# Summing pairs of state products with an accumulating transfer before TensorE adds them, in the selective-scan stage of a four-layer network

## The chip, the cores and the metric

The kernel runs on one core of one Trainium2 chip. The metric is the device time of one execution in microseconds, median over several runs. Everything is computed in float32.

## The reference, cut to what matters

The network has four layers, each an attention-like part and a feed-forward part with a residual and a layer norm. The change lies in the last layer's first part, a selective state-space recurrence. With 4 batches of 1024 tokens, 256 channels `e` and 16 states `n` it computes

```python
def step(h, inp):
    d_l, b_l, c_l, x_l = inp
    h = jnp.exp(d_l[:, :, None] * A) * h + (d_l * x_l)[:, :, None] * b_l[:, None, :]
    y_l = jnp.einsum('ben,bn->be', h, c_l)
    return (h, y_l)
_, ys = lax.scan(step, h0, (delta, Bm, Cm, xs))
y = ys.transpose(1, 0, 2) + xs * W_D
```

So for each state `n` there is a linear recurrence over the tokens for every channel. Its result is multiplied by `C[n]`, and the 16 products are summed. After that come a gate, a projection, a layer norm, and the last feed-forward part, a mixture of eight experts of width 512 that are all computed and weighted by a gate.

## The kernel before, in words

The program is written with pools of named tiles. Each pool has a number of buffers per name. A scheduler that estimates times fixes the order of the instructions on each engine when the program is built; on the chip each engine then works through its own queue in that order, and semaphores hold an instruction until its inputs are there and its output buffer is free.

The last layer is worked off in eight halves: four batches, two halves of 512 tokens each. Three pieces of code make up a half:

- `l3_prepare` (L1613) norms the input, projects it (`pxe`), applies the convolution, projects to delta, B and C (`pdb`, then `pd`), and leaves `dl` (delta, 128 channels x 2 x 512), `ud` (delta times x, the same shape) and, in DRAM, `rows`: 16 rows of B and 16 of C. The last matmuls of it on TensorE (PE) are `pd` at L1694; VectorE (DVE) writes `ud` at L1709.
- `l3_scan` (L1713) loops over the 16 states. For each it loads a row of B and a row of C, broadcast to 128 partitions, on SyncE's queue (`bn` and `cn`, L1734, 256 KB each, four buffers). GpSimd (POOL) multiplies `ud` with `bn` into `db` (L1739, four buffers). ScalarE (ACT) makes the decay `da` with an exponential (L1743). DVE runs the recurrence along the tokens in place in `db` (L1744). POOL multiplies `db` with `cn` into `hc` (L1755, 128 x 1024, 512 KB, four buffers). PE sums: with an identity as the fixed matrix, two matmuls per state, one per 128 channels, add `hc` into two PSUM banks `pys` that stay open over the 16 states (`add`, L1724, recorded at L122, the line of the helper `mm`). The add of state `n - 1` is issued after the product of state `n`.
- `l3_finish` (L1766) gates and projects the result, norms it, and puts the half on a list for the last feed-forward part.

`l3` (L1514) weaves them: while the scan of a half is written down state by state, each step also takes one piece of the preparation of the next half, one piece of the finish of the half before and some pieces of side work. The side work (`l3_side`, L1565) is first the rest of the mixture of experts of the layer before (with its gathers by POOL, `yg`, L1468), then `l3_ffn` (L1835), the last feed-forward part of halves that are finished: matmuls `ph`, Relu on ACT (`hh`, L1848), matmuls `py`, and a weighted sum on DVE (`h_acc`, L1864). What is left of it after the last scan ends the program.

Of the kernel before, what the change touches and what calls it, by code (L numbers as in the profile page):

```python
# [14 lines left out]
ALU = mybir.AluOpType  # L15
# [25 lines left out]
E3, NST, DDELTA, KCONV = 256, 16, 64, 4  # L41
# [17 lines left out]
class Net:  # L59
# [1653 lines left out]
    def l3_scan(self, u):  # L1713


        nc, c3, b, h = self.nc, self.c3, u["b"], u["h"]
        sp, wp, aneg = c3["sp"], c3["wp"], c3["aneg"]
        wout = c3["we"][:, :, ND:]
        xnT, xs, dl, ud, rows = (u[k] for k in ("xnT", "xs", "dl", "ud", "rows"))
        carry = wp.tile([P, 2, NST], F32, name="carry") if h == 0 else u["prev"]["carry"]  # L1720
        u["carry"] = carry
        py = [self.psb(f"y{ec}", [P, 512], f"pys{ec}") for ec in range(2)]

        def add(n, hc):  # L1724
            for ec in range(2):
                self.mm(py[ec], self.ident, hc[:, ec, :], n == 0, n == NST - 1)

        last = None
        for n in range(NST):
            bc = []  # L1730
            for i, nm in enumerate(("bn", "cn")):
                t = wp.tile([P, 1, 512], F32, name=nm, bufs=4)
                r = i * NST + n
                nc.sync.dma_start(  # L1734
                    out=t[:, 0, :], in_=rows[r : r + 1, :].to_broadcast([P, 512])
                )
                bc.append(t.to_broadcast([P, 2, 512]))
            db = wp.tile([P, 2, 512], F32, name="db", bufs=4)
            nc.gpsimd.tensor_mul(db, ud, bc[0])  # L1739
            for ec in range(2):  # L1740
                j = ec * NST + n
                da = self.psb("da", [P, 512], "da")
                nc.scalar.activation(da, dl[:, ec, :], AF.Exp, scale=aneg[:, j : j + 1])  # L1743
                nc.vector.tensor_tensor_scan(  # L1744
                    db[:, ec, :],
                    da,
                    db[:, ec, :],
                    carry[:, ec, n : n + 1] if h else 0.0,
                    ALU.mult,
                    ALU.add,  # L1750
                )
            if h == 0:
                nc.scalar.copy(carry[:, :, n : n + 1], db[:, :, 511:512])
            hc = wp.tile([P, 2, 512], F32, name="hc", bufs=4)
            nc.gpsimd.tensor_mul(hc, db, bc[1])  # L1755
            if last is not None:
                add(n - 1, last)
            last = hc
            yield
        add(NST - 1, last)  # L1760
        for ec in range(2):
            nc.vector.scalar_tensor_tensor(
                xs[:, ec, :], xs[:, ec, :], self.col("W_D", i=ec), py[ec], ALU.mult, ALU.add
            )
# [317 lines left out]
```

## Time and profile before

| | us |
|---|---|
| median of 3 runs | 2528.93 |
| lowest, highest | 2528.28, 2533.65 |
| own time of the profiled execution | 2467.89 |
| its span, first to last instruction | 2466.1 |
| PE busy | 2154.3 (87%) |
| DVE busy, ACT busy | 1447.0 (59%), 1355.3 (55%) |
| POOL busy | 817.9 (33%) |
| `db` products on POOL, 128 of 2.37 us | 299.6 |
| `hc` products on POOL, 128 of 2.37 us | 299.8 |
| `pys` matmuls on PE, 512 records of 0.62 us | 247.1 |

A 512-wide float32 matmul leaves two records, so the 256 adds show as 512. Records of one engine overlap a little; back to back, one record follows another of this shape after 0.43 us. The profile is of one execution, on the core's own clock; PE's granted clock was 0.921 of full speed over the span. The scans begin at 1442.6 us, and the last `pys` add is at 2315.8 us.

### The profile page before, as it was taken

To read this page: it belongs to the slowest core of one execution; us is meant where nothing else is said; L and a number is where in the kernel's file an instruction comes from. 1 tells how busy PE (TensorE), PEld (TensorE's weight loads), DVE (VectorE), ACT (ScalarE), POOL (GpSimd) and SP (SyncE) were. 2 spreads that over 40 slices of the span, in tenths; PEclk is the share of its full clock that TensorE was granted. 3 is DMA by queue.
4 is the path that set the end of the run, shared out by engine and by line. 5 is a ranking of instruction groups with operands and counts; after the bars stand their busy time and mean duration, and the time that the engine had idled before them with its cause. 6 is when DMAs were issued, how large, how long until landed. Compare 5 with 4: busy or idle time off the path is not lost.

```text
span 2466.1 us, 34752 instructions
## 1 busy us (share of the span) xinstructions
PE 2154.3 (87%) x12026; PEld 1447.0 (59%) x12026; DVE 1447.0 (59%) x4119; ACT 1355.3 (55%) x2917; POOL 817.9 (33%) x509
## 2 busy tenths in 40 slices
PE   6677888888999999999999768866999999999988
PEld 2455654534677777777776434433566555555656
DVE  7448744323566756756665467767775657666431
ACT  6642433422666656565654676666756565656443
POOL 5002310000000020020012287778792938568300
PEclk9667989989999999999999978886999999899989
DMA  3001100001400000000002243343332222313000
GB/s 99 0 18 26 30 26 9 9 9 46 150 1 1 1 14 6 5 13 4 7 13 83 65 135 103 106 148 102 83 83 61 82 70 73 94 54 120 22 5 5
DMA packets 110431, 122.27 MB, mean 50 GB/s; under 512 B 15477, under 2 KB 72816, under 8 KB 109872
## 3 DMA queue, kind: packets, MB, share of 16 engines
q1 hardware_dynamic: 103728, 106.23, 14.9%
q0 software_dynamic: 5376, 9.62, 1.4%
q10 hardware_dynamic: 1152, 4.19, 0.5%
q8 instruction: 97, 1.59, 0.3%
q14 instruction: 78, 0.64, 0.1%
HBM read 96.85 MB, written 23.16 MB: 49 GB/s over the span
## 4 chain that ended last, share of the span: by engine, by line
PE 62%; DVE 18%; ACT 11%; issue 5%; DMA 3%; POOL 1%; SPq 0%; DVEq 0%; ACTq 0%; POOLq 0%
PE ph L122 13%; PE py L122 9%; PE pys L122 6%; PE po L1086 4%; PE po L122 4%; PE pt L126 3%; DVE db L1744 3%; PE pqk L122 3%; PE po L1102 3%; PE pr L122 2%; PE pv L122 2%; PE pst L122 2%; DVE num L1122 2%; DVE a L1075 1%; PE pa L122 1%
## 5 line engine op out<-in xcount | busy, mean ns | idle before, releaser
L1739 POOL TENSOR_TENSOR db<-ud,bn 128x1024 f32<-128x1024 f32 x128 | 299.6, 2373 | 187.4 <-DVE ud L1709 105.2
L1755 POOL TENSOR_TENSOR hc<-db,cn 128x1024 f32<-128x1024 f32 x128 | 299.8, 2371 | 41.7 <-DVE db L1744 26.6
L122 PEld LDWEIGHTS py<-wH,hh 128*128 128x128 f32 x2048 | 251.1, 193 | 77.3 <-issue 46.1
L122 PE MATMUL py<-wH,hh 128*128 128x128 f32 x2048 | 257.3, 278 | 11.5 <-ACT hh L1848 10.8
L122 PE MATMUL ph<-xT,wH 128*128 128x512 f32 x512 | 258.8, 623 | 7.0 <-DVE ln_nm L161 3.6
L122 PE MATMUL pys<-hc,sb_c_ident 128*128 128x512 f32 x512 | 247.1, 616 | 17.6 <-POOL hc L1755 17.6
L1122 DVE SCALAR_TENSOR_TENSOR num<-po,sb_c_trig,nsin 128x65 f32<-128x65 f32 x512 | 132.4, 278 | 210.9 <-ACT nsin L1119 210.5
L1119 ACT ACTIVATE nsin<-po,sb_c_trig 128x65 f32<-128x65 f32 x512 | 148.3, 316 | 188.9 <-DVE num L1122 113.3
L1848 ACT ACTIVATE hh<-ph,sb_cols 128x512 f32<-128x512 f32 x256 | 171.0, 681 | 136.3 <-PE ph L122 110.2
L1743 ACT ACTIVATE da<-dl,aneg 128x512 f32<-128x512 f32 x256 | 175.8, 690 | 84.4 <-DVE db L1744 83.5
L122 PEld LDWEIGHTS pys<-hc,sb_c_ident 128*128 128x128 f32 x512 | 97.6, 198 | 125.0 <-issue 104.1
L996 POOL MEMSET cv<- 128x16 f32 x32 | 4.0, 127 | 501.4 <-ACT cv L1013 310.6
L1744 DVE TENSOR_TENSOR_SCAN db<-da,db 128x512 f32<-128x512 f32 x128 | 149.3, 1206 | 31.0 <-POOL db L1739 16.6
L1744 DVE TENSOR_TENSOR_SCAN db<-da,carry,db 128x512 f32<-128x512 f32 x128 | 155.7, 1265 | 16.9 <-POOL db L1739 12.1
L1864 DVE SCALAR_TENSOR_TENSOR h_acc<-py,gt,h_acc 128x128 f32<-128x128 f32 x256 | 71.8, 342 | 136.6 <-PE py L122 136.4
L122 PEld LDWEIGHTS ph<-xT,wH 128*128 128x128 f32 x512 | 93.4, 200 | 93.5 <-issue 67.3
L122 PE MATMUL pqk<-xT,wE 128*128 128x256 f32 x512 | 137.4, 391 | 9.4 <-DVE cv L1006 6.1
L1338 POOL DMA_INDIRECT xrows<-xN,di x64 | 61.7, 964 | 235.8 <-ACT kN L1040 162.7
L1086 PE MATMUL po<-cv,a 128*128 128x130 f32 x1024 | 136.2, 275 | 1.9 <-DVE num L1122 1.9
L1086 PEld LDWEIGHTS po<-cv,a 128*128 128x128 f32 x1024 | 125.2, 191 | 3.9 <-PE pst L122 1.1
L126 PE MATMUL pt<-sb_c_ident,xN 128*128 128x128 f32 x256 | 64.4, 353 | 71.1 <-ACT xN L165 50.1
L122 PE MATMUL ph<-wF,xgT 128*128 x184 | 107.6, 671 | 13.5 <-ACT mhT L1435 7.8
(425 smaller groups left out, 4372.8 us busy)
## 6 DMA issues: line engine op xcount, KB each, us to landing
bn<-rows SPq DMA_DIRECT2D x128, 256.0 KB, 3.4
cn<-rows SPq DMA_DIRECT2D x128, 256.0 KB, 3.3
xrows<-zero SPq DMA_DIRECT2D x4, 1472.0 KB, 11.9
xg<-xrows SPq DMA_DIRECT2D x20, 256.0 KB, 2.9
yrows<-ys SPq DMA_DIRECT2D x20, 256.0 KB, 2.4
wH<-in_wH ACTq DMA_DIRECT2D x8, 512.0 KB, 6.4
wF<-in_wF SPq DMA_DIRECT2D x1, 3072.0 KB, 16.4
xN<-in_x SPq DMA_DIRECT2D x8, 256.0 KB, 4.7
```

The source lines that it names most:

```text
L122: return self.nc.tensor.matmul(out=out, lhsT=lhsT, rhs=rhs, start=start, stop=stop)
L126: self.nc.tensor.transpose(out, in_, self.ident[0:n, 0:n])
L1086: self.nc.tensor.matmul(out=u["po"][i][:, c, :], lhsT=u["a"][:, i, c, :], rhs=Q["v"][c][:, 2 * hp + i, :, :].rearrange("p a d -> p (a d)") ...
L1102: self.nc.tensor.matmul(out=u["po"][i][:, c, :], lhsT=u["q"][h, s], rhs=Q["st"][h, hp, c, :], start=False, stop=True, skip_group_check=True,)
L1119: nc.scalar.activation(t, po[i][:, c, VW : 2 * VW], AF.Copy, scale=trig[:, k, 1:2])
L1122: nc.vector.scalar_tensor_tensor(num[:, c, i, :], po[i][:, c, 0:VW], trig[:, k, 0:1], t, ALU.mult, ALU.add)
L1739: nc.gpsimd.tensor_mul(db, ud, bc[0])
L1743: nc.scalar.activation(da, dl[:, ec, :], AF.Exp, scale=aneg[:, j : j + 1])
L1744: nc.vector.tensor_tensor_scan(db[:, ec, :], da, db[:, ec, :], carry[:, ec, n : n + 1] if h else 0.0, ALU.mult, ALU.add,)
L1755: nc.gpsimd.tensor_mul(hc, db, bc[1])
L1848: nc.scalar.activation(ht, ph, AF.Relu, bias=self.col("h_b1", i=e * NK + k))
L1864: nc.vector.scalar_tensor_tensor(acc[:, c, :], py[:, c, :], gt[:, c, e : e + 1], acc[:, c, :], ALU.mult, ALU.add,)
```

## The change

The products of two states that follow each other are now added first. After the second of the two products, POOL issues a transfer from the second `hc` tile onto the first one (`prev`), which adds in place of overwriting (`accum_op=ALU.add`). PE then adds the first tile, which holds the sum, into `pys`. There are eight such adds per half in place of sixteen. The add of a pair is issued two states later than the pair's transfer, and those that are left are issued after the loop.

```diff
         def add(n, hc):
             for ec in range(2):
-                self.mm(py[ec], self.ident, hc[:, ec, :], n == 0, n == NST - 1)
-
-        last = None
+                self.mm(py[ec], self.ident, hc[:, ec, :], n == 1, n == NST - 1)
+
+        sums = []
+        prev = None
         for n in range(NST):
...
             hc = wp.tile([P, 2, 512], F32, name="hc", bufs=4)
             nc.gpsimd.tensor_mul(hc, db, bc[1])
-            if last is not None:
-                add(n - 1, last)
-            last = hc
-            yield
-        add(NST - 1, last)
+            if n % 2:
+
+                nc.gpsimd.dma_start(out=prev, in_=hc, accum_op=ALU.add)
+                sums.append((n, prev))
+            prev = hc
+            if sums and sums[0][0] <= n - 2:
+                add(*sums.pop(0))
+            yield
+        for p in sums:
+            add(*p)
```

Nothing else differs in the source. The scheduler sees other instructions, so the built order of the last stage differs on every engine.

## The prediction

> **What bounds the kernel now.** I read the engine totals first, then the last stage cut at the starts of its eight scans (one per half of a batch), then the chain, then the rows of what the change touches.
>
> ```profile
> PE 2154.3 (87%) x12026; PEld 1447.0 (59%) x12026; DVE 1447.0 (59%) x4119; ACT 1355.3 (55%) x2917; POOL 817.9 (33%) x509
> ```
> TensorE is the busiest engine overall. Now the stage: time, then PE, PEld, DVE, ACT and POOL busy, PE clock, DMA share, GB/s.
>
> ```profile
> core 0: us, PE busy (x) PEld busy (x) DVE busy (x) ACT busy (x) POOL busy (x), PEclk, DMA share, GB/s
> 1442.60:1536.70 94.10, 77.40 (x244) 40.20 (x245) 69.96 (x108) 62.20 (x137) 75.24 (x33) 0.85 0.41 115
> 1536.70:1673.70 137.00, 95.97 (x347) 53.68 (x348) 94.72 (x174) 86.73 (x185) 104.74 (x65) 0.83 0.40 125
> 1673.70:1771.50 97.80, 82.49 (x311) 45.90 (x310) 72.15 (x125) 69.51 (x128) 74.90 (x32) 0.85 0.32 89
> 1771.50:1895.00 123.50, 118.64 (x557) 76.24 (x555) 77.80 (x148) 76.21 (x124) 74.08 (x33) 0.99 0.26 71
> 1895.00:2014.70 119.70, 111.40 (x520) 69.97 (x520) 75.98 (x147) 77.11 (x143) 74.05 (x33) 0.99 0.28 76
> 2014.70:2125.50 110.80, 103.73 (x441) 62.53 (x440) 73.64 (x136) 66.98 (x112) 73.98 (x33) 0.92 0.29 80
> 2125.50:2231.40 105.90, 100.07 (x446) 61.66 (x445) 71.42 (x131) 65.65 (x115) 74.05 (x32) 0.97 0.28 83
> 2231.40:2316.00 84.60, 83.37 (x393) 53.04 (x391) 56.88 (x99) 48.37 (x74) 74.02 (x32) 1.00 0.25 75
> 2316.00:2466.00 150.00, 130.05 (x697) 91.87 (x696) 34.99 (x128) 58.88 (x94) 0.00 (x0) 0.92 0.02 6
> ```
> Two regimes. In halves 0 to 2 (beside the experts) PE is 70 to 84% busy and POOL 77 to 80%. From half 3 on PE is at 93 to 99%, while POOL needs a constant 74 us per half and then waits:
>
> ```profile
> 1836.25 9.31 POOL L1755 TENSOR_TENSOR hc<-db,cn 128x1024 f32<-128x1024 f32 x4
> 1894.96 9.30 POOL L1739 TENSOR_TENSOR db<-ud,bn 128x1024 f32<-128x1024 f32 x4 [49.40 <-DVE ud L1709]
> ```
> It idles 49 us because ud of the next half is late, and ud is late because its matmuls stand in PE's queue behind FFN work. So PE sets the late halves. One early wait goes the other way: PE stands for hc around the start of the third scan (waits from 1630 to 1700 us).
>
> ```profile
> PEld pys L122 <- POOL hc L1755: 19.0, 3, 14.7
> ```
>
> **What the Trainium skill says.** "DMA: Bandwidth & Descriptors", section "SWDGE vs HWDGE vs iDMA": a transfer that accumulates can be issued from GpSimd only, in software. No run here has one; the indirect gathers (L1468) are the nearest. "Collectives: The Full Stack", "The bandwidth ceiling: the fold count and why AG ≠ RS ≠ AR": an add in the DMA engine costs no cycles of its own, but needs two reads per write, so it runs at half the rate of a copy. No trace here shows it. The DMA page, "Anatomy of one DMA — SWDGE (gpsimd) path", prices such a transfer at 2.0 us plus bytes/436e3. The gather of 64 KB comes to 2.15 by this; the trace has 2.6, which I use.
>
> **The change part by part.** (1) Adds on PE. A state's add is four records of 0.43 us:
>
> ```profile
> 1846.88 1.72 PE pys L122 x4
> ```
> 128 states become 64 pairs: 64 x 1.72 = 110 us of PE work gone, 41 in halves 0 to 2 and 69 in halves 3 to 7.
>
> (2) The new transfer. Each of 64 reads 512 KB of hc and 512 KB of prev, and writes 512 KB. Its nearest rows:
>
> ```profile
> L1468 POOL DMA_INDIRECT yg<-yrows,di x64: 940/945/988, 1359.4 to 1668.8; - x64
> ...
> DMA to landing us min/median/max: 2.4/2.6/6.7
> ...
> orows<-vmr SPq DMA_DIRECT2D x4, 512.0 KB, 3.2
> ...
> rows<-db SPq DMA_DIRECT2D x8, 64.0 KB, 1.7
> ```
> Issue: 0.94 us plus the 0.30 between two, 1.25 us of POOL, 10 us per half. Upper bound 3 us (more descriptors per row, since two tensors are read); below 0.9 nothing here goes. Landing L, from issue: rows and orows give 1.5 us for 448 KB, 3.3 us per MB. From the 2.6 of a 64 KB gather, 960 KB more to read is 3.2: L = 5.8 alone. While a scan runs the loads of bn and cn hold about 0.44 of the DMA engines, so the same 3.2 becomes 5.7, L = 8.3. I take 7 and keep 5 to 12: an adder slower than a copy would be above 8.3.
>
> (3) What waits for it. POOL's built order in a late half is: transfer k, db, odd hc, db, even hc, transfer k+1. That even hc takes the buffer that transfer k reads (hc has four), so it waits for L. A pair takes 4 x 2.31 (9.3/4) + 1.25 = 10.5 us as long as L is below 1.25 + 3 x 2.31 = 8.2; above, L + 2.3. **This is the hinge.** Queued behind that even hc are the next transfer and all later db, then DVE's scans. PE's add waits for the landing, with FFN matmuls and the next half's pdb and pd behind it. ACT's order holds the exponentials of five states past a pair before the first Relu that depends on matmuls behind the pair's add, so a PE wait doesn't stop POOL.
>
> (4) Moves. The scheduler rewrites the order. Summing PE's rows with their durations (0.86 us per 512-wide matmul, 0.22 per 128-wide one), PE work from one half's pd to the next is, halves 3 to 4, 4 to 5, 5 to 6, 6 to 7: 119, 106, 94, 94 before; 104, 96, 76, 80 after. The next half's pd now stands after the sixth pair of eight (halves 3, 5, 6) or the eighth (4), where it stood after all sixteen states: next half's preparation starts earlier. In half 1, 14 gathers (14 x 1.25 = 17.5 us) stand ahead of one pair's transfer; the same gathers lay inside this scan before. ACT and DVE have the same work in another order; SP issues the same 256 loads, later where POOL is later, four buffers deep: no cost while POOL takes 10.5 us for the two states of a pair.
>
> **The sum**, L = 7, from pd to scan start 16 us (measured 14.4, 14.6, 17.7).
> - Starts of half 0 to half 3, 328.9 us: up to where PE waits for POOL, two halves of issues, 20, and one landing, 7: +27. From there to half 3's pd PE has 37 us of work in place of 57, times 1.15 (the late intervals run 4 to 18% over PE's work): -23. Net +4.
> - 3 to 4: 123.5 before. PE alone: 104 x 1.04 = 108. The loop by POOL: 16 + 78 (ten products and two issues to the first transfer, five pairs) + 7 + 10 of FFN ahead of pd = 111. Take 112.
> - 4 to 5: 119.7 before; loop 16 + 83 + 7 + 4 = 110.
> - 5 to 6 and 6 to 7: 110.8 and 105.9 before; PE 76 x 1.18 and 80 x 1.13, both 90; loop 16 + 71 + 7 + 3 = 97 each.
> - 7 to the end: 234.6 before; POOL 83 + 7 + 2, then the last FFN, 150 x 114/119 (PE work after the last add) = 144: 236.
>
> Late sum 652 against 694.5: -42. PE and POOL are now within 7 us of each other in every interval, so a delay of either shows; I add 4 us per half, 20. Total 4 - 42 + 20 = **-18 us**. Own time of the profiled execution 2467.9 (1.8 around the span of 2466.1): 2450. The median of the runs is 61 us above that; the same -18 gives **2511**.
>
> **Rivals.** (B) Transfer becomes the bound, slower. It decides at L = 8.4. Each us above 8.2 lengthens 29 late pair steps, 16 early ones and six landings, 51 us in all; from 7 to 8.2 only the landings grow (+7, to -11). L = 9.3 gives -11 + 56 = +45, 2574; L = 10 gives 2610. For: DMA share is already 0.40 in halves 0 and 1, and no row shows an adding transfer. Against: 5.8 alone, and bn and cn come in bursts.
> (C) Issue is dear: 3 us, so 1.75 x 45 steps = +79 on top, 2590. For: POOL would go from 74 to 98 us per half. Against: gathers of 128 rows take 0.94.
> (D) Freed PE time turns fully into waits for pairs: 2529. For: POOL's 84 us exceeds PE's 76 and 80 in the last halves. Against: the 30 to 49 us that POOL idles between scans now.
> (E) L = 5 and PE sets everything: late intervals 108, 108, 93, 93, 232 with no extra, -60, early +2, less some: 2475. That it doesn't do what it says is out: the built program has 128 matmuls of pys, not 256.
>
> **How the numbers follow.** A with E 0.48, of which 0.46 lie below -0.2%; D 0.10, 0.01 of it faster, 0.08 same; B 0.31; C 0.11, where 0.02 of these are same. Faster 0.47, same 0.10, slower 0.43; 0.2%, 5 us, is what this measurement can tell from no change (its runs span 5.4). Both signs hold much of the chance: A alone is 2478 to 2524. The range for all, 2480 to 2622, leaves out L above 10.2 and the lowest of E.
>
> **What would show it.** Right: pys at 256 records and about 110 us; transfers landing in 6 to 8 us, 1.25 us apart from POOL's work; POOL's idle before ud below 25 us per half; scan starts about 97 to 112 us apart. Wrong: even hc waiting for the transfer (a landing above 8.4), PE idle before pys by more than 5 us per pair, or scan starts over 115 us apart.

## The result, and the profile after

The changed kernel takes 2500.98 us (median of 4 runs, 2495.84 to 2507.25), the kernel before 2528.61 on the same chip: a ratio of 0.9888, with an interval of 0.986 to 0.9916, or 28 us less. The forecast was 18 us less.

The kernel before took about 2528 us in the first two series of runs and about 2468 us in the two later ones, as in its own profiled execution; some 50 us of that lie ahead of the first scan (1491.0 against 1442.6 us), so kernels are compared at the same level only (lower: 2468, upper: 2528), and why there are two levels is not known.

The engine totals and the DMA queue from the page of the changed kernel, in microseconds and share of the span:

```profile
PE 2087.7 (83%) x11770; PEld 1425.0 (57%) x11770; DVE 1460.1 (58%) x4119; ACT 1353.9 (54%) x2918; POOL 874.1 (35%) x573
...
q0 software_dynamic: 14592, 43.18, 8.3%
...
L122 PE MATMUL pys<-hc,sb_c_ident 128*128 128x512 f32 x256 | 135.4, 655 | 25.1 <-DMA hc<-hc 25.1
```
`pys` has half its records and 135.4 us in place of 247.1: 112 us of PE work are gone. PE's total fell by less, 91 us at the same level (2178.4 in a second profile of before), so the other matmuls took longer; the granted clock of the span was 0.893 in place of 0.910. The queue that only carried gathers (5376 packets, 1.4%) now has 14592 packets and 8.3%. The last number is new: PE stood 25 us for landings of the transfer (its weight loads, PEld, stood over much the same stretches).

The last stage of the changed kernel, cut at its scan starts; the columns are time, busy time of PE, PEld, DVE, ACT and POOL, PE clock, DMA share and GB/s:

```profile
1494.10:1584.20 90.10, 63.37 (x215) 34.45 (x216) 69.29 (x111) 69.11 (x147) 76.74 (x37) 0.80 0.54 144
1584.20:1742.70 158.50, 86.29 (x319) 49.41 (x317) 100.90 (x185) 92.21 (x193) 110.40 (x73) 0.74 0.49 134
1742.70:1839.00 96.30, 69.95 (x258) 39.69 (x258) 71.74 (x108) 57.19 (x107) 81.47 (x41) 0.81 0.57 139
1839.00:1958.20 119.20, 111.26 (x538) 72.89 (x539) 82.44 (x152) 76.18 (x127) 87.59 (x45) 0.99 0.50 123
1958.20:2075.80 117.60, 102.83 (x490) 67.24 (x489) 74.97 (x147) 77.10 (x142) 81.29 (x40) 0.93 0.45 113
2075.80:2174.40 98.60, 87.17 (x399) 55.25 (x398) 72.28 (x135) 66.28 (x112) 81.10 (x41) 0.93 0.53 132
2174.40:2268.90 94.50, 81.41 (x395) 52.62 (x394) 72.74 (x131) 63.80 (x112) 81.04 (x41) 0.92 0.54 137
2268.90:2364.80 95.90, 86.00 (x411) 56.09 (x410) 62.47 (x111) 54.34 (x87) 80.98 (x40) 0.94 0.46 113
2364.80:2505.00 140.20, 122.57 (x676) 88.14 (x674) 32.86 (x118) 53.72 (x84) 0.00 (x0) 0.93 0.02 4
```
In the late halves PE has fallen from 93 to 99% of the interval to 86 to 93%, and POOL has gone from 74 to 81 to 88 us per half. In the last three halves both now stand at about 81 to 87 us of 95 to 99. The share of the DMA engines went from 0.28 to about 0.5.

The intervals against the forecast. The lower level pairs the profile of before (span 2466.1) with a second profile of the changed kernel (span 2443.3); the upper level pairs a second profile of before (span 2529.3) with that of the changed kernel (2505.3).

| us | forecast | before, after (lower level) | change | before, after (upper level) | change |
|---|---|---|---|---|---|
| half 0 to 3 | +4 | 328.9, 335.9 | +7.0 | 339.8, 345.0 | +5.2 |
| 3 to 4 | -11.5 | 123.5, 119.2 | -4.3 | 122.1, 119.2 | -2.9 |
| 4 to 5 | -9.7 | 119.7, 115.6 | -4.1 | 122.4, 117.6 | -4.8 |
| 5 to 6 | -13.8 | 110.8, 99.7 | -11.1 | 111.1, 98.6 | -12.5 |
| 6 to 7 | -8.9 | 105.9, 94.6 | -11.3 | 106.2, 94.5 | -11.7 |
| 7 to the end | +1.4 | 234.6, 235.9 | +1.3 | 236.7, 236.4 | -0.3 |
| allowance | +20 | | | | |
| sum | -18.5 | | -22.5 | | -27.0 |

POOL in a late half of the changed kernel (start and duration in us):

```profile
1906.26 2.36 POOL L1756 TENSOR_TENSOR hc<-db,cn 128x1024 f32<-128x1024 f32 x1
1908.57 0.83 POOL L1759 DMA_DIRECT2D hc<-hc  x1
1909.15 2.65 POOL L1740 TENSOR_TENSOR db<-ud,bn 128x1024 f32<-128x1024 f32 x1
1911.47 2.62 POOL L1756 TENSOR_TENSOR hc<-db,cn 128x1024 f32<-128x1024 f32 x1
1913.79 2.62 POOL L1740 TENSOR_TENSOR db<-ud,bn 128x1024 f32<-128x1024 f32 x1
1916.11 2.61 POOL L1756 TENSOR_TENSOR hc<-db,cn 128x1024 f32<-128x1024 f32 x1
1918.40 1.16 POOL L1759 DMA_DIRECT2D hc<-hc  x1
1918.97 2.96 POOL L1740 TENSOR_TENSOR db<-ud,bn 128x1024 f32<-128x1024 f32 x1
```
The record of the issue lasts 0.8 to 1.2 us, and the next product starts 0.58 us after it (1908.57 to 1909.15), so the records overlap. But that is not all that the issue costs. The products behind it last longer, 2.65 us in place of 2.36, and 2.96 behind the next transfer. These later ends are real, for what depends on a product starts with them: here a scan on DVE starts 0.03 us after a product that lasted 3.05 us (the bracket is the idle time before, with what ended it).

```profile
1754.78 3.05 POOL L1740 TENSOR_TENSOR db<-ud,bn 128x1024 f32<-128x1024 f32 x1
1757.86 2.34 DVE L1745 TENSOR_TENSOR_SCAN db<-da,db 128x512 f32<-128x512 f32 x2 [5.30 <-POOL db L1740]
```
From the product behind one transfer to that behind the next are 9.82 us by their starts and 10.13 by their ends (1911.80 to 1921.93), and four products without a transfer take 9.25. So an adding transfer costs POOL about 0.9 us, 0.58 of which show in the starts. The busy time agrees: 81.1 us per half in place of 74.0 is 7.1 for eight transfers.

Waits of the changed kernel, first PE up to 1842 us (halves 0 to 2), then POOL from there to the last scan's end (who waited for whom: us in all, times, longest):

```profile
PE pys L122 <- DMA hc<-hc: 22.9, 4, 10.9
```
```profile
POOL db L1740 <- ACT dl L1710: 36.3, 2, 26.1
POOL db L1740 <- DVE ud L1709: 29.9, 2, 19.9
POOL hc L1756 <- PE pys L122: 19.5, 7, 5.1
```
Of PE's 25 us, 23 lie before half 3; in the late halves it hardly stands for a landing. POOL's idle time for the next half's `dl` and `ud` is 66 us over four halves there, where before it was 163. The third line is new there: the product that takes over the tile with a pair's sum waits until PE has read it.

### The profile page after: what moved, and what is told of

Its sections match the earlier page's. It is cut to its first block, busy times and chain, and to the rows that moved or that the text cites. A ratio compares the mean times of both kernels' runs of the same rounds, so it can differ in the third digit from the quotient of the medians.

```text
span 2505.3 us, 34222 instructions
## 1 busy us (share of the span) xinstructions
PE 2087.7 (83%) x11770; PEld 1425.0 (57%) x11770; DVE 1460.1 (58%) x4119; ACT 1353.9 (54%) x2918; POOL 874.1 (35%) x573
## 3 DMA queue, kind: packets, MB, share of 16 engines
q0 software_dynamic: 14592, 43.18, 8.3%
## 4 chain that ended last, share of the span: by engine, by line
PE 59%; DVE 18%; ACT 11%; issue 6%; DMA 3%; another core or an unknown queue 1%; POOL 1%; SPq 0%; ACTq 0%; DVEq 0%; POOLq 0%
PE ph L122 13%; PE py L122 9%; PE po L1086 4%; PE po L122 4%; PE pt L126 4%; DVE db L1745 3%; PE pqk L122 3%; PE po L1102 3%; PE pys L122 2%; PE pv L122 2%; PE pr L122 2%; PE pst L122 2%; DVE num L1122 2%; DVE a L1075 1%; PE pa L122 1%
## 5 line engine op out<-in xcount | busy, mean ns | idle before, releaser
L1740 POOL TENSOR_TENSOR db<-ud,bn 128x1024 f32<-128x1024 f32 x128 | 346.8, 2797 | 72.3 <-ACT dl L1710 36.3
L1756 POOL TENSOR_TENSOR hc<-db,cn 128x1024 f32<-128x1024 f32 x128 | 331.8, 2720 | 90.6 <-PE pys L122 27.7
L122 PE MATMUL pys<-hc,sb_c_ident 128*128 128x512 f32 x256 | 135.4, 655 | 25.1 <-DMA hc<-hc 25.1
L1338 POOL DMA_INDIRECT xrows<-xN,di x64 | 61.8, 965 | 235.9 <-ACT kN L1040 165.3
L126 PEld LDWEIGHTS pt<-sb_c_ident,xN 128*128 128x128 f32 x256 | 43.0, 183 | 124.7 <-ACT xN L165 86.6
```

What stands on the lines that cost most here:

```text
L122: return self.nc.tensor.matmul(out=out, lhsT=lhsT, rhs=rhs, start=start, stop=stop)
L126: self.nc.tensor.transpose(out, in_, self.ident[0:n, 0:n])
```

## The experiments

The kernel before and the changed kernel were run again as controls.

> The kernel before, unchanged, for a profile on the same chip as the runs below. The profile shown so far began its scans at 1442.6 us and had a span of 2466.1, 61 us under the median of its runs; the changed kernel's profile began them at 1494.1. If the 51 us lie in that one execution, this profile starts its first scan at about 1490 to 1505 us and has a span of about 2526, with 1025 to 1035 us from there to the end. If the changed order costs them ahead of the first scan, this one starts at about 1445 again.

> The changed kernel again, beside the others: 25 to 30 us under before, 2498 to 2504 us.

> The changed kernel once more, to stand beside the others of this call. The earlier ratio to the kernel before was 0.989 with an interval of 0.986 to 0.992; theory: the same, 0.986 to 0.992, though the kernel before may take another time here than the 2528 of the first measurement.

Measured: before 0.9993 of itself (0.9974 to 1.0013). The changed kernel 0.9893 (0.9861 to 0.9924) at the upper level and 0.9919 (0.9896 to 0.9943) at the lower, where it took 2447.78 us against 2468.33. The intervals overlap. Lower-level runs below are compared with these two numbers; before took 2468.95 in the other lower-level series.

**The transfer left out, and sixteen adds beside it.** Two edits of the changed kernel: in the first, the transfer's line is deleted, so only the eight even products of a half are summed; in the second, the transfer stays and PE adds both tiles, so that it makes sixteen adds (the second product of a pair then counts twice).

```diff
# first
-                nc.gpsimd.dma_start(out=prev, in_=hc, accum_op=ALU.add)
# second
-                self.mm(py[ec], self.ident, hc[:, ec, :], n == 1, n == NST - 1)
+                self.mm(py[ec], self.ident, first[:, ec, :], n == 1, False)
+                self.mm(py[ec], self.ident, second[:, ec, :], False, n == NST - 1)
...
-                sums.append((n, prev))
+                sums.append((n, prev, hc))
```

> The changed kernel without the accumulating transfer; PE adds the eight even products alone, so half of the sum is left out. Theory (fewer adds pay, the transfer lies within the slack of the four hc buffers): POOL loses 64 x 0.58 us of issue and PE its 25 us of waits for landings, so 10 to 25 us under the changed kernel, 2475 to 2492 us. Rival (the transfer eats a large part of what PE gains): 40 us or more under it, below 2460 us. Rival (the gain is the new order's alone): within 5 us of the changed kernel.

> The changed kernel with the transfer, but PE adds both tiles of each pair, sixteen adds again (the second product of each pair is counted twice). Theory (fewer adds pay): 64 x 1.72 = 110 us of PE work are back, 69 of them in the halves where PE sets the pace, and the transfer is still to be waited for: 2530 to 2555 us. Rival (the new order of pairs and late adds is what pays): it stays within 10 us of the changed kernel, 2495 to 2511 us.

Measured: 2461.19 us, ratio 0.9733 (0.9702 to 0.9765), without the transfer; 2551.01, ratio 1.0094 (1.006 to 1.0128), with sixteen adds. With before and after these make a square, all at the upper level:

| us | no transfer | transfer |
|---|---|---|
| sixteen adds | 2528.5 (before) | 2551.0 |
| eight adds | 2461.2 | 2501.2 (after) |

Eight adds fewer are worth 67 us without the transfer and 50 with it, out of 110 us of PE work. The transfer costs 22 us where PE makes sixteen adds and 40 where it makes eight, which fits that more of the transfer shows where PE is less the bound. So the gain is of the adds, and the transfer takes over half of it. My theory put the transfer's price too low: its range for the first run ended at 2475.

**Only the order.** Sixteen adds, issued in pairs two states later, without a transfer.

```diff
+                self.mm(py[ec], self.ident, first[:, ec, :], n == 1, False)
+                self.mm(py[ec], self.ident, second[:, ec, :], False, n == NST - 1)
...
-                nc.gpsimd.dma_start(out=prev, in_=hc, accum_op=ALU.add)
-                sums.append((n, prev))
+                sums.append((n, prev, hc))
```

> Sixteen products are added by PE, as before, but in pairs and two states later, as the changed kernel does, and there is no transfer. Theory (the gain comes from the adds that PE no longer makes, order counts little): 2520 to 2532, within 8 us of the kernel before, and 18 to 30 us below the run with both the transfer and sixteen adds (2551), since the transfer's price is gone. Rival (adds that stand later free the next half's preparation and the products, and that is what pays): 2500 to 2510.

Measured: 2466.22 us against 2468.95, ratio 0.9985 (0.9975 to 0.9994). The absolute figures of the expectation are of the upper level; within its level the run is 3 us below before, so later adds alone bring almost nothing, and the rival falls.

**A plain copy in place of the adding transfer.** The even products are overwritten. The built order is the same as the changed kernel's on every engine, so this difference is of the hardware alone.

```diff
-                nc.gpsimd.dma_start(out=prev, in_=hc, accum_op=ALU.add)
+                nc.gpsimd.dma_start(out=prev, in_=hc)
```

> The transfer from POOL overwrites the even product in place of adding to it, so the eight even products of each half are left out of the sum; issue, waits and adds of PE stay. Theory (the transfer costs by its issue and its waits, the adding itself costs nothing): within 6 us of the changed kernel (2501), landing within 0.5 us of that of the adding transfer. Rival (the adding, with its second read, makes the landing late and takes DMA time from the loads of bn and cn): 2480 or less, landing 1.5 us earlier or more.

Measured: 2436.61 us, ratio 0.9867 (0.9851 to 0.9884), 11 us below the changed kernel. The DMA queue from this kernel's page:

```profile
q0 software_dynamic: 14592, 43.18, 4.8%
```
Its issues and its products do not have the later ends: the issue is 0.57 us, and POOL is busy for 78.6 to 78.9 us in halves 4 to 6, 4.6 to 4.9 more than before for eight copies.

```profile
L1759 POOL DMA_DIRECT2D hc<-hc x64 | 36.5, 570 | 1.2 <-POOL hc L1756 1.2
```
With before's 1.4% of gathers (0.014 x 2466 = 35 us) taken off, 64 copies held the 16 engines for 0.048 x 2433 - 35 = 82 us, 1.3 us each; 64 adding transfers held them for 0.083 x 2505 - 35 = 173 us, 2.7 us each. The adding doubles the transfer's DMA time. The Trainium skill ("Collectives: The Full Stack", section "The bandwidth ceiling: the fold count and why AG ≠ RS ≠ AR") says of the adding step of a collective that it takes about twice a copy because it reads two sources; the factor here, 2.1, agrees, while the second read itself is not seen in the trace. From the packet records of that queue, the last packet of an adding transfer is done a median of 5.8 us after the issue (4.2 the shortest), that of the copy 4.6 (2.6 the shortest). Both expectations were off: the adding is not free, and it costs half of what the rival named. It changes three things at once (DMA time, landing, and 0.3 us more of POOL per transfer), and how the 11 us divide among them is open. Interval by interval, 3 to 4 and 4 to 5 stay at 119.1 and 115.5 us (119.2 and 115.6), while 0 to 3, 5 to 7 and the last scan give 6.7, 3.9 and 2.3 us: in these two intervals a landing 1.2 us later and POOL's 0.3 us cost nothing.

**The copy from SP's queue, and adds that need not wait.** The first moves the plain copy to SyncE. The second keeps the adding transfer, but PE adds the odd tile, which is there before the transfer starts. Both leave the even products out of the sum.

```diff
# first
-                nc.gpsimd.dma_start(out=prev, in_=hc, accum_op=ALU.add)
+                nc.sync.dma_start(out=prev, in_=hc)
# second
-                sums.append((n, prev))
+                sums.append((n, hc))
```

> A plain copy, issued on SP's queue in place of POOL's; the eight even products of each half are left out. Theory (POOL's issue and the ring of four hc buffers cost most of the 40 us that the transfer costs): 2465 to 2485 if the issue is most of it, with POOL's pair cycle 0.6 us shorter. Rivals: the landing and the bytes cost, 2495 to 2503, the same as a copy from POOL; or SP's loads of bn and cn, which now queue behind a copy that waits for its product, come late and hold the products on POOL: 2520 or more.

> The adding transfer stays, but PE adds the odd tile, which is ready before the transfer starts, so PE never waits for a landing; the even products are left out of the sum. The ring of hc still waits for the landing. Theory A (PE's waits for landings, 56 us in the trace of the changed kernel from the first scan on, are what the transfer costs): 2475 to 2490. Theory B (the issue on POOL and the even product that waits for its buffer cost, and PE's waits are made up later): 2496 to 2503.

Measured: 2424.26 us, ratio 0.9813 (0.9797 to 0.983), and 2423.28 us, ratio 0.9813 (0.9796 to 0.9829): 24 us below the changed kernel each, and the first 12 below the copy from POOL. The DMA issues of the copy from SP:

```profile
bn<-rows SPq DMA_DIRECT2D x128, 256.0 KB, 3.4
cn<-rows SPq DMA_DIRECT2D x128, 256.0 KB, 4.1
hc<-hc SPq DMA_DIRECT2D x64, 512.0 KB, 3.1
```
The copy lands after 3.1 us (from POOL 4.9 by the same view), and four products back to back, start to start, take 9.25 us on POOL in place of 9.81: the copy's issue of 0.57 us per pair is gone. The rival of late loads, a slower run, is out. Both ratios are what the theories said (the 56 us of the second one sum PE's waits and those of its weight loads, which cover much the same time; PE stood 25). But the two gains can't be added up: the scheduler built another order on every engine for both. In the run with the odd tile, 16 us are gained up to the last `pd` of half 2 (84 and 134 us from `pd` to `pd` become 78 and 123), where PE of the changed kernel stood for landings. Another 11 us are gained from the `pd` of half 4 to that of half 5 (114 to 104), where it hardly did, and 15 are lost again in the two halves behind. That part goes with the order. So PE's waits for landings and POOL's issue are likely to hold much of the 29 us that the adding itself doesn't explain (40 less 11), but with the order changed too, neither share is shown.

**Pairs in the late halves only.** Halves 0 to 2 add sixteen products as before.

```diff
+        pairs = b > 1 or (b == 1 and h == 1)
+        first = 1 if pairs else 0
...
+            if pairs:
+                if n % 2:
+                    nc.gpsimd.dma_start(out=prev, in_=hc, accum_op=ALU.add)
+                    sums.append((n, prev))
+                if sums and sums[0][0] <= n - 2:
+                    add(*sums.pop(0))
+            else:
+                if prev is not None:
+                    add(n - 1, prev)
+                if n == NST - 1:
+                    sums.append((n, hc))
```

> Pairs and transfers only from half 3 on; halves 0 to 2 add sixteen products as before. Theory (in halves 0 to 2 POOL and the experts set the time, so there the transfers cost, 5 us by the scan starts, and the freed PE time is worth nothing): 3 to 9 us below the changed kernel, ratio to before 0.985 to 0.988. Rival (the 41 us of adds that PE is spared in halves 0 to 2 let the work of the late halves start earlier): 8 us above the changed kernel or more.

Measured: 2441.55 us (2440.24 to 2445.37), ratio 0.9892 (0.987 to 0.9914), 6 us below the changed kernel (2444.68 to 2452.71); the intervals of the two ratios overlap. It computes the whole result, and its median is the lowest of the runs that do. Half 0 to half 3 takes 329.5 us, as before the change (328.9), in place of 335.9: the 41 us of PE adds that come back there cost nothing, and 24 transfers were a loss. From half 3 to the end it takes 665.9 us, as the changed kernel does (665.0).

**A ring of three.** `hc` has three buffers, and a pair's add is issued right behind its transfer.

```diff
-            hc = wp.tile([P, 2, 512], F32, name="hc", bufs=4)
+            hc = wp.tile([P, 2, 512], F32, name="hc", bufs=3)
...
-            if sums and sums[0][0] <= n - 2:
+            if sums and sums[0][0] <= n:
```

> The ring of hc has three buffers in place of four, and the add of a pair is issued right behind its transfer. The product two places after a transfer then takes the buffer that the transfer writes and PE reads, so it waits for a landing (6 us) and PE's add (1.7 us). Theory (a landing of 6 us leaves the ring of four a reserve of about 2 us, a product's time, which this takes away; POOL's pair cycle goes from 9.8 to 10.5 to 12 us and the loop sets the late halves): 10 to 45 us above the changed kernel. Rival (the ring plays no part, waits for hc are a sign of late PE only): within 5 us of the changed kernel.

Measured: 2461.07 us, ratio 0.9964 (0.9949 to 0.9979), 13 us above the changed kernel, inside the theory's range. But not where the theory put it. Its waits over the whole span:

```profile
PEld pys L122 <- DMA hc<-hc: 68.1, 23, 10.2
PE pys L122 <- DMA hc<-hc: 55.1, 19, 8.6
POOL hc L1756 <- PE pys L122: 53.9, 20, 16.7
```
PE's waits for landings and POOL's for buffers have about doubled. Half 0 to half 3 takes 357.1 us in place of 335.9, and from half 3 to the end it is 663.0 in place of 665.0. The scheduler's order differs too, so that the ring alone is not shown; with both, the early halves lose 21 us and the late ones nothing.

**The pair added by DVE.** No transfer; DVE adds the odd product to the even one a state later.

```diff
+            if n % 2 == 0 and n:
+                nc.vector.tensor_add(pair[0], pair[0], pair[1])
+                sums.append((n - 1, pair[0]))
             if n % 2:
-                nc.gpsimd.dma_start(out=prev, in_=hc, accum_op=ALU.add)
-                sums.append((n, prev))
+                pair = (prev, hc)
...
+        nc.vector.tensor_add(pair[0], pair[0], pair[1])
+        sums.append((NST - 1, pair[0]))
```

> No transfer: DVE adds the two products of a pair, one state later, and PE adds the sum. Eight adds of 128x1024 per half, each about 1.4 us (twice the 0.69 us of a 128x512 add from SBUF), are 11 us of DVE per half, where DVE is busy 75 of about 110 us. Theory (what the transfer costs is its landing and its issue on POOL; an add of 1.4 us on an engine with time to spare has neither): near the run without the transfer, ratio to before 0.972 to 0.980, 20 to 40 us below the changed kernel. Rival (DVE waits for POOL's odd product in its own order, and the scans behind it come late; or the adds slow POOL's products in SBUF): the same as the changed kernel or slower, 0.988 or more.

Measured: 2468.71 us, ratio 0.9995 (0.9982 to 1.0008): the whole gain is gone. The add's row, then POOL's products in the same kernel (min/median/max in ns):

```profile
L1758 DVE TENSOR_TENSOR hc<-hc x56: 1194/2520/3366, 1460.7 to 2316.0; 128x1024 f32<-128x1024 f32 x56
```
```profile
L1756 POOL TENSOR_TENSOR hc<-db,cn x128: 2331/2354/3365, 1453.2 to 2313.4; 128x1024 f32<-128x1024 f32 x128
```
And both engines around 1930 us, DVE first:

```profile
1928.16 1.10 DVE L1873 SCALAR_TENSOR_TENSOR h_acc<-py,gt,h_acc 128x128 f32<-128x128 f32 x4
1929.18 2.69 DVE L1758 TENSOR_TENSOR hc<-hc 128x1024 f32<-128x1024 f32 x1
1931.80 2.33 DVE L1745 TENSOR_TENSOR_SCAN db<-da,db 128x512 f32<-128x512 f32 x2
1934.04 1.19 DVE L1758 TENSOR_TENSOR hc<-hc 128x1024 f32<-128x1024 f32 x1
```
```profile
1928.43 2.36 POOL L1756 TENSOR_TENSOR hc<-db,cn 128x1024 f32<-128x1024 f32 x1
1930.74 6.71 POOL L1740 TENSOR_TENSOR db<-ud,bn 128x1024 f32<-128x1024 f32 x2
1937.41 2.35 POOL L1756 TENSOR_TENSOR hc<-db,cn 128x1024 f32<-128x1024 f32 x1
```
The add alone takes 1.19 us. Issued at 1929.18 beside a product, it ends at 1931.87, 1.1 us after that product's end (1930.79); and the two products that follow on POOL take 6.71 us in place of 4.65, since this add and a second one, at 1934.04, each hold one back for about 1 us. The engines take turns, and POOL's 256 products together last 650 us in place of 605 in the run without the transfer. The Trainium skill says it, on the page "SBUF — State Buffer", section "SBUF: two separate sides": a DVE operation with two inputs in SBUF and a GpSimd operation that reads SBUF exclude each other for the whole instruction. The trace agrees. The recurrence on DVE, with one input in PSUM, shows nothing of it: 1.18 to 1.28 us throughout. How the 21 us above the changed kernel divide between slower products, scans that start later and PE's waits for the add (24 us) was not taken apart.

## Why the prediction was right, point by point

The total came out near, -22.5 and -27.0 for -18.5, in part by luck: a step was wrong by 13 us, and the allowance of 20 us, put at 4 us in each half, covered it.

- **PE adds, 110 us.** Measured 112 by the rows. Right, and the square shows that 50 of them came through.
- **Issue, 1.25 us.** POOL pays 0.9: the pair cycle is 10.1 us by the products' ends, not 10.5. The term was taken from the gather's record plus the gap behind it; the record alone, 0.94, would have been near.
- **Landing, L = 7.** 5.8 us in the median, 4.2 for the shortest (forecast 5.8 alone), about 7 for the slowest tenth. All but the slowest lie below the hinge (with the issue as measured, 0.9 + 3 x 2.31 = 7.8), so rival B did not come up. The base was too high: I started from the gather's 2.6 us; the price of "DMA: Bandwidth & Descriptors", section "Anatomy of one DMA — SWDGE (gpsimd) path", 2.0 us plus bytes/436e3, is an estimate of 4.4 if both reads (1.049 MB) are counted, near the shortest landing of 4.2.
- **The hinge at 8.2 us.** The ring of three takes its reserve away, and the late intervals don't move. So the price of 51 us per us above 8.2, most of it in late halves, is not borne out; a landing above 8.2 itself was not tried. The hinge also left something out: the even product takes the tile that the transfer reads, but the odd one behind it takes the tile with the sum, and waits for PE to read it. "A PE wait doesn't stop POOL" does not hold: from half 3 on POOL stood 19.5 us for `pys`, and not at all in the profile of before.
- **Halves 0 to 3, +4.** +7.0 and +5.2. The run with pairs in the late halves only shows the sign: 6.4 us come back. The size is near, but its parts are not as forecast: 16 issues are 14 us in place of 20, and PE stood 22.9 us for landings where one of 7 was counted.
- **3 to 4 and 4 to 5, -11.5 and -9.7.** This is the step that failed: -4.3 and -4.1 (-2.9 and -4.8 at the upper level). For 3 to 4 I took PE's work times 1.04, the factor of before (108, and 112 with POOL's loop). From the last `pd` of half 3 to that of half 4, `pys` fell from 72 records to 44 (12 us of PE), with the same number of the other matmuls, but the time fell only from 122.0 to 119.6. PE's waits took 7 us of the 12 back. The rest is longer matmuls (`py` 41.7 us in place of 39.7 for 346 records; the granted clock was 0.986 there, before 1.000). PE's waits in that stretch, before and then after:

```profile
PE py L122 <- ACT hh L1848: 1.4, 1, 1.4
PE ph L122 <- DVE h_acc L1864: 0.4, 1, 0.4
```
```profile
PE ph L122 <- DVE h_acc L1870: 3.5, 1, 3.5
PE py L122 <- ACT hh L1854: 3.4, 3, 2.1
PE ph L122 <- ACT hh L1854: 1.8, 1, 1.8
PE ph L122 <- DVE xs L1675: 0.2, 1, 0.2
```
No landing is among them. PE now stands for Relu and for the weighted sum of the FFN, 8.9 us in place of 1.8; before, adds stood in PE's queue at such places and filled them. From scan start to scan start the factor is 119.2/104 = 1.15. The run without the transfer points the same way: with 40 records in this stretch PE stands 5.9 us in place of 2.0, though no transfer is there to wait for. It still takes 113.2 us, so the transfer costs there too without a wait of PE for a landing. No run put the filling back alone, so this is a reading of the waits, not a test. For 4 to 5 I took POOL's loop, 110, but POOL stood 26 us for `dl` at its end. From `pd` to `pd` 12 us of adds went there too, and PE's waits rose from 8.4 to 13.8 us, at a clock of 0.956 in place of 0.986.
- **5 to 6 and 6 to 7.** -11.1 and -11.3 against -13.8 and -8.9; there I had 1.18 and 1.13 for PE. `pd` does stand after the sixth pair, and PE and POOL are equally long, as forecast.
- **7 to the end, +1.4.** +1.3 and -0.3.
- **Allowance, 20.** At the lower level the intervals are 16 us above the sum without it, but 13 of those are the two intervals just named, not 4 in each half.
- **Signs.** POOL's idle time before `ud` and `dl` is 17 us per half (below 25). The sign of a wrong forecast, scans over 115 us apart, is there in two intervals, although the whole is faster. PE's waits of 25 us for 64 pairs stay below 5 us per pair.
- **Rivals.** D (freed time turns into waits) is true of the two intervals, with Relu in the landing's place; as a whole it would have given 2529. C falls with the issue's 0.9 us.

## What to carry to other kernels

Work taken from the busiest engine is worth its duration only as far as that engine stays the bound and its queue has other work ready: here 110 us of matmuls gave 67 us, of which the replacement took 40. Put such a replacement only in the stages where the relieved engine is the bound; the same edit lost 6 us in the three halves where it was not. Before a sum is moved to another engine, look at what runs beside it there: the add that looked cheapest, 1.2 us on DVE, excluded POOL's products and lost the gain. And read the price of an instruction from the ends of what follows it too, not from the starts alone.

## What was not expected of the hardware

- An adding transfer of 512 KB within SBUF costs POOL 0.9 us of its time, a plain copy 0.57. The difference does not show in the starts of the products behind it but in their ends, and it grows with each transfer until POOL waits for something. The transfer holds the DMA engines 2.7 us in place of 1.3, and it lands after 5.8 us beside other loads.
- A plain copy of the same tile lands 1.8 us earlier from SP's queue than from POOL's (3.1 against 4.9).
- A DVE add of 128x1024 takes 1.19 us alone and 2.5 beside POOL's products.
